# Where the expert products of a routed feed-forward stand: three ups for two gates in the route, and block 4's ups at fixed places in block 3's end

## The chip, the core and the metric

The kernel runs on one core of a Trainium2 chip. Five engines work side by side, each through its own queue in order: TensorE (PE) multiplies and transposes into PSUM, VectorE (DVE) and ScalarE (ACT) read PSUM and SBUF, GpSimd (POOL) works on SBUF, SyncE (SP) issues DMAs. ACT can issue DMAs too; such an issue stands in ACT's queue like any other instruction. Engines wait for one another through semaphores. The metric is the device time of one execution in microseconds. Three runs of the kernel before took 1309.42, 1313.48 and 1315.73 us; the median is 1313.48.

## What is computed

Four blocks one after the other on x, 2 sequences of 1024 tokens with 128 features, each with a residual: two attention layers with a feed-forward, two local attention layers with a gated feed-forward, one attention with local heads and a latent path mixed by a gate (block 3), and a routed feed-forward of 64 experts with 32 hidden units each (block 4). The change touches the end of block 3 and the first half of block 4. Cut to that:

```python
# block 3, end
gate = jax.nn.sigmoid(local @ gl_w + remote_h @ gr_w)
mixed = gate * local + (1.0 - gate) * remote_h
x = x + (mixed @ out_w + out_b)

# block 4, on the layernorm of x
router_scores = jax.nn.softmax(xt @ Wr + br, axis=-1)        # 2048 tokens x 64 experts
order = jnp.argsort(-router_scores, axis=0)                  # tokens sorted for each expert
group_score = sorted_vals.reshape(Tq, 64, En).sum(axis=1)    # groups of 64 sorted tokens
_, top_flat = jax.lax.top_k(group_score.reshape(-1), Tq * 16)
fs = jnp.where(mask, router_scores, 0.0)                     # scores of the chosen groups
fs = fs / (fs.sum(axis=-1, keepdims=True) + 1e-06)
up = jnp.einsum('td,edh->teh', xt, Wup) + bup
gate = jnp.einsum('td,edh->teh', xt, Wgate) + bgate
h = jax.nn.silu(up) * gate * fs[:, :, None]
out = jnp.einsum('teh,ehd->td', h, Wdown) + fs @ bdown
```

`up` and `gate` do not depend on the routing, so they can be computed while the routing sorts and searches. `h` needs the routing's result, and `out` needs `h`.

## The kernel before

The matmuls and vector operations are written out by hand in the order in which each engine shall take them; in blocks 3 and 4 no scheduler moves them.

**Block 3** runs in beats. `both` (L1030) makes four beats; in each it lets the `Pipe` (L109) run what is due, then one of the score, transpose and value steps of the attention tiles, then one step of `front.todo`, the sort passes that are ready. `Pipe.later(beats, f, bank, rank)` sets a step some beats ahead; with `bank` true it moves on to the next beat that is free for a PSUM bank; within a beat, steps run by rank, lower first. When all eight heads' values of a tile are there, `finish` (L1260) copies them to SBUF (`oT`, L1263) and sets `rest`, which transposes them back (L1270) and normalises them (L1273, L1276). When a group of tiles is complete, `gate` (L1360) weighs local against remote (L1375 to L1399), transposes (L1406), multiplies by the output weights (L1412) and adds to `xo` (L494). For the very last group (`last`) these steps run on DVE at once. Then `Front.tiles` (L1477) normalises the new tokens for block 4: statistics on DVE (L166, L167), the root on POOL (L168 to L171), the scaling (L173) on POOL, on DVE for the last group only. It goes on to transposes (L1490) copied into `xTd` (L1491), router scores (L1496, L1503 to L1507), exp (L1510), softmax weights (L1515 to L1517), transposes of these (L1530), and their copy with a sign into `r_zab` (L1534), from which the sort begins. Each group adds its sort passes to `front.todo`; a pass is a maximum (L1460) and a minimum (L1461) on DVE.

When the tile loop is over, a drain loop calls `both` with a list `todo`: nothing for nine beats, then `ex.up(2)` in six of nine beats. These are the first 12 of the experts' 64 ups.

**The experts' first half** (`Experts`, L1560): there are 64 ups and 64 gates, each one matmul of 128 columns by 512 tokens in float32 (two PE instructions in the trace, L1597). An up is passed through silu on ACT into `hid` (L1606). A gate stays in its PSUM bank until DVE multiplies it into `hid` (L1620); I call this the product. In the route four banks of PSUM, `big`, serve ups and gates. `feed` keeps up to three gates ahead of DVE (four once the ups are gone). `fill(n)` n times issues one product, one up and what `feed` finds room for.

**The route** (`route`, L1741) is a chain on DVE with `fill` calls set into it: the rest of `front.todo`, first 128- and 256-wide passes, then (L1780) ten 512-wide passes, a swap of the two halves by two DMAs (L1786 on SP, L1787 on ACT's queue) and its use at L1793, four more 512-wide passes (L1795), group sums and minima (L1807, L1816), a search in five steps (L1826, whose costly part is L1831), small selections with short PE operations in between (L1849, L1862 to L1864, L1882, L1892), two comparisons over all scores (L1906, L1907), a running sum (the scan L1914) and the masking of the scores (L1919 to L1927). `split` (L1755) cuts the scores into three bfloat16 parts on the way (L1758 on ACT, L1761 on DVE). Only when the masks are there does the second half of block 4 begin: totals (L1683), weighing (L1656, L1660), down (L1672) and the stores.

Of the kernel before, what the change touches and what calls it, by code (L numbers as in the profile page):

```python
# [31 lines left out]
NB = 2  # L32
MT = S // P
# [934 lines left out]
class BlockC:  # L968
# [27 lines left out]
    def run(self):  # L996
        pipe = self.pipe

        def latent():
            self.latent_keys(0)  # L1000
            self.prep(1, 0, 6, lambda: self.prep(1, 1, 10, lambda: self.latent_keys(1)))

        self.prep(0, 0, 1)
        self.prep(0, 1, 9, latent)
        while pipe.now < 8:
            pipe.beat()
        tiles = [(b, at + i) for at, n in self.GROUPS for b in range(NB) for i in range(n)]
        self.mask(*tiles[0])
        for n, (b, m) in enumerate(tiles):
            if m > 4 and m % 2:  # L1010
                self.latent(b, m - 1)
            for ip in range(2):
                nxt = tiles[n + 1] if ip and n + 1 < len(tiles) else None
                self.both(b, m, ip, nxt)

        turn = itertools.cycle(("s0", "s1"))

        def bank():
            for tag in turn:
                wide = self.k.ps_c.tile([P, 1024], F32, tag=tag, name=self.k.name("big"))  # L1020
                yield wide[:, :512]
                yield wide[:, 512:]

        self.ex.bank = bank().__next__
        up, none = lambda: self.ex.up(2), lambda: None
        todo = [none] * 9 + [up, up, none, up, up, none, none, up, up]
        while self.turns or self.values or pipe.due:
            self.both(todo=todo)

    def both(self, b=None, m=None, ip=None, nxt=None, todo=None):  # L1030

        now = self.score(b, m, ip) if m is not None else []
        todo = todo if todo is not None else []
        for i in range(4):
            self.pipe.beat()
            for f in now[i : i + 1] + self.turns[i : i + 1] + self.values[i : i + 1]:
                f()
            if nxt and i == 0:
                self.mask(*nxt)
            for fs in (self.front.todo, todo):  # L1040
                for f in fs[:1]:
                    f()
                del fs[:1]
        for f in self.values[4:]:
            self.pipe.later(0, f)
        self.values = self.turns[4:]
# [213 lines left out]
    def finish(self, b, m):  # L1260
# [18 lines left out]
            )  # L1279
            self.done(b, m)  # L1280

        self.pipe.later(1, rest, True)

    def latent(self, b, m):

# [71 lines left out]
            (2, True, out),  # L1357
        )

    def gate(self, b, j):  # L1360

        k, nc, st = self.k, self.k.nc, self.st[b]
# [20 lines left out]
        def sums():  # L1383
            for i in range(2):
                nc.vector.tensor_reduce(gs[:, i, : n * 16], pws[i], AX.X, ALU.add)
            nc.vector.tensor_tensor(g, g, gs[:, 1, : n * 16], ALU.add)
            if last:
                tanh()
                eng.tensor_tensor(local, local, remote, ALU.subtract)

        def tanh():
            nc.scalar.activation(g, g, AF.Tanh, scale=0.5)
# [16 lines left out]
        def out():  # L1409
            ps = k.mm()  # L1410
            for i in range(n):
                nc.tensor.matmul(  # L1412
                    ps[:, i * D : (i + 1) * D], mT[:, i * P : (i + 1) * P], k.c_out,
                    start=True, stop=True,
                )
            add_tiles(k, k.xo[:, b * MT + at : b * MT + at + n], ps[:, : n * D])
            self.front.tiles(self.pipe, b, at, n)

        beats = (0, 0, 1, 1, 1) if last else (1, 2, 1, 3, 2)
        steps = ((False, products), (False, sums), (False, mix), (True, features), (True, out))  # L1420
# [43 lines left out]
class Front:  # L1464
# [12 lines left out]
    def tiles(self, pipe, b, at, n):  # L1477
# [2 lines left out]
        t = slice(b * MT + at, b * MT + at + n)  # L1480
        xn = w.tile([P, 4, D], F32, tag="xnd", name=k.name("xn"))[:, :n]
        last = (b, at) == (NB - 1, 6)
        norm_tiles(k, w, k.xo[:, t], xn, n, nc.vector if last else nc.gpsimd)
        cut = self.xT[:, b * S + at * P : b * S + (at + n) * P]
        sc = self.sc[:, at : at + n, b, :]

# [73 lines left out]
class Experts:  # L1560
# [6 lines left out]
    def __init__(self, k, xT, own):  # L1567
# [2 lines left out]
        self.parts = [(tp, h) for tp in range(2) for h in range(NB)]  # L1570
        self.units = [(tp, h, c) for tp, h in self.parts for c in range(8)]
        halves = [(unit, e) for unit in self.units for e in range(2)]
        self.ups, self.gates, self.ready = list(halves), list(halves), []

    def new(self):
        n, k = len(self.hid), self.k
# [48 lines left out]
    def fill(self, n=1):  # L1625

        for _ in range(n):
            if self.ready:
                self.ready.pop(0)()
                self.up()  # L1630
                self.feed()


# [107 lines left out]
def route(k, p1, front, fill):  # L1741
# [5 lines left out]
    nc = k.nc  # L1747
# [19 lines left out]
    for n, f in enumerate(front.todo):  # L1767
# [3 lines left out]
            next(first)  # L1771
        elif left == 6:
            next(second)
        fill(n % 2 if left < 10 else n % 3 > 0)

    za, zb = zab[:, 1, :], zab[:, 0, :]

# [2 lines left out]
    j = 512  # L1780
    while j >= 1:
        sort_pass(k, za, zb, 1024, j, j == 512)
        fill()
        za, zb = zb, za
        j //= 2
    nc.sync.dma_start(zb[:64, :], za[64:, :])  # L1786
# [8 lines left out]
    j = 512  # L1795
    while j >= 64:
        sort_pass(k, za, zb, 1024, j, False)
        fill()
        za, zb = zb, za
        j //= 2  # L1800

# [24 lines left out]
    for step in (8, 4, 2, 1, 0):  # L1826
# [2 lines left out]
            pick, k.sm("lrank", 0, 16), n, gs, ALU.is_equal, ALU.mult, accum_out=piv  # L1829
        )  # L1830
        nc.vector.tensor_scalar(junk, every, piv, None, ALU.is_gt, ALU.add, accum_out=above)  # L1831
        fill()
        if step:
            nxt = step // 2 if step > 1 else 1

# [11 lines left out]
    nc.vector.tensor_tensor(piv, piv, above, ALU.add)  # L1847
    ps = k.tr()
    nc.tensor.transpose(ps[:, :P], piv.to_broadcast([P, P]), k.ident)  # L1849
    fill(3)  # L1850
    nc.vector.tensor_reduce(low, ps[:, :P], AX.X, ALU.min)


# [8 lines left out]
    nc.tensor.matmul(ps[:, :2], k.mat["ones"], cnt, start=True, stop=True)  # L1862
    nc.tensor.matmul(ps[:, 2:18], k.mat["tri"], eq, start=True, stop=True)
    nc.tensor.matmul(ps[:, 18:34], k.mat["blk"], eq, start=True, stop=True)  # L1864
    fill(3)
    cs = new([P, 34], "cs")
    nc.vector.tensor_copy(cs, ps[:, :34])
    inc = new([P, 16], "inc")
# [11 lines left out]

    ps = k.mm()
    nc.tensor.matmul(ps[:, :1], k.mat["pair"], cnt[:, 0:1], start=True, stop=True)  # L1882
    fill(3)
    num = new([P, 1], "num")
    nc.vector.tensor_copy(num, ps[:, :1])
    thr = new([P, 1], "thr")
# [6 lines left out]
    none = new([P, 1], "none")  # L1893
    nc.vector.tensor_scalar(none, num, 0.0, 9.0, ALU.is_equal, ALU.mult)
    v = new([P, 1], "v")
    fill(3)
    both = junk[:, :P]
    nc.vector.scalar_tensor_tensor(
        both, ps[:, :P], 1.0, k.mat["pair"], ALU.mult, ALU.mult, accum_out=v
# [270 lines left out]
```

## Time and profile before

One execution was profiled. Its own time is 1315.62 us; the span from the first to the last instruction is 1313.7 us.

| what | us |
|---|---|
| time of the profiled execution | 1315.62 |
| busy over the span: PE, DVE, ACT, POOL | 1153.0, 867.7, 645.3, 485.6 |
| last output transposes of block 3 (L1270) start | 1070.09 |
| sign copy L1534 starts | 1093.02 |
| first product L1620 starts | 1099.64 |
| first 512-wide pass starts | 1138.60 |
| scan L1914 starts | 1219.52 |
| totals L1683 start on PE | 1226.07 |

Busy time of the end, by stage, of the same execution (us):

| stretch | length | PE | DVE | ACT | granted PE clock |
|---|---|---|---|---|---|
| 1000 to 1066, last attention tiles | 66 | 56.8 | 57.5 | 41.9 | 0.95 |
| 1066 to 1092, end of block 3 | 26 | 18.9 | 17.3 | 14.6 | 0.87 |
| 1092 to 1142, 128- and 256-wide passes | 50 | 39.4 | 48.5 | 16.8 | 0.93 |
| 1142 to 1176, 512-wide passes | 34 | 33.7 | 33.2 | 14.7 | 1.00 |
| 1176 to 1194, search | 18 | 13.8 | 17.4 | 5.6 | 1.00 |
| 1194 to 1226, selection, scan, masks | 32 | 24.0 | 25.9 | 5.5 | 0.96 |
| 1226 to 1314, second half of block 4 | 88 | 83.4 | 48.2 | 0.0 | 0.96 |

How to read such views: busy time of PE is modelled at its end, since matmuls overlap, so the distance from one start to the next says more than the duration. An engine takes its queue in order, so a wait at one instruction holds everything behind it. A wait is put down to the engine that released it last. The granted clock is the share of full speed that PE's clock was given in a stretch.

### The profile page before, as it was taken

How to read it: one execution, taken by the hardware profiler on the slowest of the kernel's cores; microseconds unless marked ns; L12 is line 12 of the kernel's file. 1: busy time of each engine (PE TensorE's matmuls, PEld its weight loads, DVE VectorE, ACT ScalarE, POOL GpSimd, SP SyncE). 2: the span in 40 equal slices, each digit the busy share in tenths (PEclk: the TensorE clock that was granted, in tenths of full speed). 3: DMA queues.
4: the chain of work that ended last, by engine and by line, in shares of the span. 5: the costliest groups of instructions: out<-in, count | busy, mean ns of one | idle time of the engine just before them, and what ended most of it. 6: DMA issues, size and time to landing. Idle time of an engine off the chain costs nothing.

```text
span 1313.7 us, 23414 instructions
## 1 busy us (share of the span) xinstructions
PE 1153.0 (88%) x9381; PEld 742.0 (56%) x9441; DVE 867.7 (66%) x1787; ACT 645.3 (49%) x1212; POOL 485.6 (37%) x559
## 2 busy tenths in 40 slices
PE   5899999997588999989989877989999967898798
PEld 3566666665345666656666634545555532243698
DVE  5566666645267776775776625656677969998763
ACT  5454545543245765655655635656665753342000
POOL 1523333223478886675786542222222210000000
PEclk9999999999799999999999988989998988999899
DMA  9000000000011100010101012000000000000000
GB/s 292 1 1 1 1 1 2 1 1 1 9 25 25 26 22 17 22 26 13 24 21 24 6 41 76 2 1 1 1 1 2 1 1 1 0 17 0 25 17 17
DMA packets 19840, 25.18 MB, mean 19 GB/s; under 512 B 2762, under 2 KB 13716, under 8 KB 19476
## 3 DMA queue, kind: packets, MB, share of 16 engines
q1 hardware_dynamic: 19076, 23.02, 6.3%
q8 instruction: 75, 1.23, 0.4%
q10 hardware_dynamic: 656, 0.66, 0.2%
q14 instruction: 33, 0.27, 0.1%
HBM read 13.32 MB, written 1.05 MB: 11 GB/s over the span
## 4 chain that ended last, share of the span: by engine, by line
PE 59%; DVE 23%; ACT 7%; POOL 5%; issue 5%; DMA 0%; DVEq 0%; POOLq 0%; ACTq 0%
PE big L1597 6%; PE mm L1672 4%; PE bank L403 4%; PE s L368 4%; PE bank L904 4%; PE qk L679 3%; PE bank L453 2%; PE s L1206 2%; PE s L779 2%; PE bank L824 2%; DVE nm L1211 2%; PE bank L471 2%; PE tr L1243 2%; DVE nm L374 2%; PE bank L391 2%
## 5 line engine op out<-in xcount | busy, mean ns | idle before, releaser
L724 POOL TENSOR_TENSOR t<-raw,tab 128x512 f32<-128x512 f32 x64 | 80.5, 1282 | 88.3 <-DVE raw L715 84.9
L1211 DVE TENSOR_REDUCE nm<-s 128x4 f32<-128x1024 f32 (+1 forms) x64 | 71.0, 1151 | 60.3 <-PE s L1206 60.0
L374 DVE TENSOR_REDUCE nm<-s 128x1 f32<-128x1024 f32 x64 | 75.1, 1216 | 51.9 <-PE s L368 51.9
L1244 ACT COPY pT<-tr 128x512 f32<-128x512 f32 x120 | 70.0, 597 | 73.2 <-PE tr L1243 73.0
L687 ACT ACTIVATE sq<-qk 128x1024 f32<-128x1024 f32 x32 | 32.7, 1023 | 97.0 <-PE qk L679 97.0
L1243 PE MATMUL tr<-ident,pr 128*128 128x128 f32 x480 | 77.1, 284 | 2.6 <-ACT pT L1244 2.3
L1606 ACT ACTIVATE hid<-big,cols 128x512 f32<-128x512 f32 x62 | 41.9, 686 | 75.8 <-PE big L1597 75.8
L737 POOL TENSOR_TENSOR raw<-raw,t 128x1024 f32<-128x1024 f32 x32 | 75.7, 2365 | 1.9
L731 POOL TENSOR_TENSOR raw<-raw,tab 128x1024 f32<-128x1024 f32 x32 | 75.4, 2355 | 2.5
L1597 PE MATMUL big<-xTd,d_gate 128*128 128x512 f32 x128 | 66.1, 610 | 11.1 <-ACT hid L1606 7.5
L1597 PE MATMUL big<-xTd,d_up 128*128 128x512 f32 x128 | 70.6, 643 | 5.3 <-DVE hid L1620 3.2
L380 ACT ACTIVATE pr<-s,nm 128x1024 f32<-128x1024 f32 x64 | 71.1, 1120 | 7.4 <-DVE nm L374 7.3
L679 PE MATMUL qk<-b_wqkv,hT 128*128 128x512 f32 x128 | 66.4, 643 | 9.4 <-POOL hT L640 5.4
L391 PEld LDWEIGHTS bank<-ident,pr 128*128 128x128 f32 x512 | 56.1, 141 | 30.1 <-issue 22.5
L403 PE MATMUL bank<-pT,v 128*64 128x128 f32 x1024 | 71.7, 284 | 0.7 <-DVE pT L396 0.2
L394 ACT COPY pT<-bank 128x512 f32<-128x512 f32 x64 | 34.9, 587 | 69.1 <-PE bank L391 69.1
L403 PEld LDWEIGHTS bank<-pT,v 128*64 128x64 f32 x1024 | 56.2, 139 | 22.1 <-issue 10.7
L1243 PEld LDWEIGHTS tr<-ident,pr 128*128 128x128 f32 x480 | 54.6, 144 | 21.2 <-issue 11.8
L368 PE MATMUL s<-kk,q 64*128 64x512 f32 x256 | 65.5, 622 | 0.6 <-ACT pr L380 0.5
L391 PE MATMUL bank<-ident,pr 128*128 128x128 f32 x512 | 65.3, 276 | 0.0
L1672 PEld LDWEIGHTS mm<-d_down,hid 128*128 128x128 f32 x496 | 60.4, 194 | 5.7 <-DVE xo L1703 1.9
L1672 PE MATMUL mm<-d_down,hid 128*128 128x128 f32 x496 | 61.1, 278 | 1.3 <-DVE xo L1703 1.3
(359 smaller groups left out, 2809.7 us busy)
## 6 DMA issues: line engine op xcount, KB each, us to landing
vs<-v SPq DMA_DIRECT2D x60, 130.0 KB, 2.2
b_wqkv<-in_L_ffn_wqkv_dram SPq DMA_DIRECT2D x2, 768.0 KB, 8.9
b_tab<-in_c_xpos_dram SPq DMA_DIRECT2D x1, 1024.0 KB, 7.9
d_up<-in_L_ffn_Wup_dram SPq DMA_DIRECT2D x1, 1024.0 KB, 5.2
d_gate<-in_L_ffn_Wgate_dram SPq DMA_DIRECT2D x1, 1024.0 KB, 9.1
out_dram<-xo SPq DMA_DIRECT2D x3, 256.0 KB, 2.3
rows<-in_rows_dram SPq DMA_DIRECT2D x1, 760.0 KB, 7.1
b_w<-in_L_ffn_w_dram SPq DMA_DIRECT2D x2, 341.0 KB, 7.2
```

Source lines behind the costliest of these rows:

```text
L368: nc.tensor.matmul(t["s"][h][:, keys], q[rows, qt * P : (qt + 1) * P], kk[rows, keys], start=True, stop=True,)
L374: nc.vector.tensor_reduce(t["nm"][h], t["s"][h], AX.X, ALU.max, negate=True)
L391: nc.tensor.transpose(ps[:, i * P : (i + 1) * P], t["pr", h][:, at : at + P], k.ident)
L403: nc.tensor.matmul(t["u"][h * 64 : h * 64 + 64, :P], v[:, kb, h * 64 : h * 64 + 64], t["pT"][:, h, kb], start=(kb == 0), stop=(kb == MT - 1),)
L679: nc.tensor.matmul(qk[:, cut], lhsT, k.b_wqkv[:, l, cut], start=True, stop=True)
L724: nc.gpsimd.tensor_tensor(t2[:, :, :, a : a + 32], r4[:, :, :, z : z + 32], self.tabs[l][1][:, m, :, None, a : a + 32].to_broadcast([P, 2, ...
L731: nc.gpsimd.tensor_tensor(r4, r4, self.tabs[l][0][:, m, :, None, :].to_broadcast([P, 2, 8, 64]), ALU.mult)
L737: nc.gpsimd.tensor_tensor(flat, flat, t["t2"].rearrange("p j h d -> p (j h d)"), ALU.add)
L1211: nc.vector.tensor_reduce(nm[h], view[h], AX.X, ALU.max, negate=True)
L1243: nc.tensor.transpose(ps[:, c * P : (c + 1) * P], pr[:, c, t * P : (t + 1) * P], k.ident)
L1597: self.k.nc.tensor.matmul(ps, weights[:, rows], self.xT[:, cut], start=True, stop=True)
L1672: nc.tensor.matmul(sums[part][:, cols], hid[tp, h, c][:, e, cols], k.d_down[:, c + 8 * e, :], start=start and e == 0, stop=False,)
```

## The change

1. The drain loop's list is gone. The 12 ups of block 3's end are set at fixed places instead: four behind the gate sums of the last group, four behind its output, and two each four and five beats later with rank 1, which is behind the transposes and scores due in these beats.
2. `rest` gets rank -1, ahead of all else in its beat, and for the last tile it no longer looks for a free beat.
3. The scaling L173 is on DVE for the last group of both sequences (`at == 6`), not of the second alone.
4. `fill` issues two ups with every odd product and one with every even one, so three ups for two gates.
5. The counts of `fill` along the route: two steps in three also in the last nine steps of `front.todo` (one in two before), one and two in turn in the 512-wide passes (one before), two in each search step (one before), two where the selections had three.

No matmul and no vector operation is added or removed; the scaling of one group moves from POOL to DVE.

```diff
--- before.py
+++ after.py
@@ -1022,25 +1022,21 @@
                 yield wide[:, 512:]
 
         self.ex.bank = bank().__next__
-        up, none = lambda: self.ex.up(2), lambda: None
-        todo = [none] * 9 + [up, up, none, up, up, none, none, up, up]
         while self.turns or self.values or pipe.due:
-            self.both(todo=todo)
-
-    def both(self, b=None, m=None, ip=None, nxt=None, todo=None):
+            self.both()
+
+    def both(self, b=None, m=None, ip=None, nxt=None):
 
         now = self.score(b, m, ip) if m is not None else []
-        todo = todo if todo is not None else []
         for i in range(4):
             self.pipe.beat()
             for f in now[i : i + 1] + self.turns[i : i + 1] + self.values[i : i + 1]:
                 f()
             if nxt and i == 0:
                 self.mask(*nxt)
-            for fs in (self.front.todo, todo):
-                for f in fs[:1]:
-                    f()
-                del fs[:1]
+            for f in self.front.todo[:1]:
+                f()
+            del self.front.todo[:1]
         for f in self.values[4:]:
             self.pipe.later(0, f)
         self.values = self.turns[4:]
@@ -1279,7 +1275,7 @@
             )
             self.done(b, m)
 
-        self.pipe.later(1, rest, True)
+        self.pipe.later(1, rest, (b, m) != (NB - 1, MT - 1), -1)
 
     def latent(self, b, m):
 
@@ -1356,6 +1352,10 @@
             (1, True, score), (1, False, exp), (1, True, turn), (2, True, value), (2, True, across),
             (2, True, out),
         )
+
+    def ups(self):
+        for _ in range(2):
+            self.ex.up(2)
 
     def gate(self, b, j):
 
@@ -1387,6 +1387,7 @@
             if last:
                 tanh()
                 eng.tensor_tensor(local, local, remote, ALU.subtract)
+                self.ups()
 
         def tanh():
             nc.scalar.activation(g, g, AF.Tanh, scale=0.5)
@@ -1415,6 +1416,11 @@
                 )
             add_tiles(k, k.xo[:, b * MT + at : b * MT + at + n], ps[:, : n * D])
             self.front.tiles(self.pipe, b, at, n)
+            if last:
+
+                self.ups()
+                for beats in (4, 5):
+                    self.pipe.later(beats, lambda: self.ex.up(2), False, 1)
 
         beats = (0, 0, 1, 1, 1) if last else (1, 2, 1, 3, 2)
         steps = ((False, products), (False, sums), (False, mix), (True, features), (True, out))
@@ -1480,7 +1486,7 @@
         t = slice(b * MT + at, b * MT + at + n)
         xn = w.tile([P, 4, D], F32, tag="xnd", name=k.name("xn"))[:, :n]
         last = (b, at) == (NB - 1, 6)
-        norm_tiles(k, w, k.xo[:, t], xn, n, nc.vector if last else nc.gpsimd)
+        norm_tiles(k, w, k.xo[:, t], xn, n, nc.vector if at == 6 else nc.gpsimd)
         cut = self.xT[:, b * S + at * P : b * S + (at + n) * P]
         sc = self.sc[:, at : at + n, b, :]
 
@@ -1570,7 +1576,7 @@
         self.parts = [(tp, h) for tp in range(2) for h in range(NB)]
         self.units = [(tp, h, c) for tp, h in self.parts for c in range(8)]
         halves = [(unit, e) for unit in self.units for e in range(2)]
-        self.ups, self.gates, self.ready = list(halves), list(halves), []
+        self.ups, self.gates, self.ready, self.filled = list(halves), list(halves), [], 0
 
     def new(self):
         n, k = len(self.hid), self.k
@@ -1627,7 +1633,8 @@
         for _ in range(n):
             if self.ready:
                 self.ready.pop(0)()
-                self.up()
+                self.filled += 1
+                self.up(1 + self.filled % 2)
                 self.feed()
 
 
@@ -1771,7 +1778,7 @@
             next(first)
         elif left == 6:
             next(second)
-        fill(n % 2 if left < 10 else n % 3 > 0)
+        fill(n % 3 > 0)
 
     za, zb = zab[:, 1, :], zab[:, 0, :]
 
@@ -1780,7 +1787,7 @@
     j = 512
     while j >= 1:
         sort_pass(k, za, zb, 1024, j, j == 512)
-        fill()
+        fill(1 + j.bit_length() % 2)
         za, zb = zb, za
         j //= 2
     nc.sync.dma_start(zb[:64, :], za[64:, :])
@@ -1795,7 +1802,7 @@
     j = 512
     while j >= 64:
         sort_pass(k, za, zb, 1024, j, False)
-        fill()
+        fill(1 + j.bit_length() % 2)
         za, zb = zb, za
         j //= 2
 
@@ -1829,7 +1836,7 @@
             pick, k.sm("lrank", 0, 16), n, gs, ALU.is_equal, ALU.mult, accum_out=piv
         )
         nc.vector.tensor_scalar(junk, every, piv, None, ALU.is_gt, ALU.add, accum_out=above)
-        fill()
+        fill(2)
         if step:
             nxt = step // 2 if step > 1 else 1
 
@@ -1847,7 +1854,7 @@
     nc.vector.tensor_tensor(piv, piv, above, ALU.add)
     ps = k.tr()
     nc.tensor.transpose(ps[:, :P], piv.to_broadcast([P, P]), k.ident)
-    fill(3)
+    fill(2)
     nc.vector.tensor_reduce(low, ps[:, :P], AX.X, ALU.min)
 
 
@@ -1862,7 +1869,7 @@
     nc.tensor.matmul(ps[:, :2], k.mat["ones"], cnt, start=True, stop=True)
     nc.tensor.matmul(ps[:, 2:18], k.mat["tri"], eq, start=True, stop=True)
     nc.tensor.matmul(ps[:, 18:34], k.mat["blk"], eq, start=True, stop=True)
-    fill(3)
+    fill(2)
     cs = new([P, 34], "cs")
     nc.vector.tensor_copy(cs, ps[:, :34])
     inc = new([P, 16], "inc")
@@ -1880,7 +1887,7 @@
 
     ps = k.mm()
     nc.tensor.matmul(ps[:, :1], k.mat["pair"], cnt[:, 0:1], start=True, stop=True)
-    fill(3)
+    fill(2)
     num = new([P, 1], "num")
     nc.vector.tensor_copy(num, ps[:, :1])
     thr = new([P, 1], "thr")
@@ -1893,7 +1900,7 @@
     none = new([P, 1], "none")
     nc.vector.tensor_scalar(none, num, 0.0, 9.0, ALU.is_equal, ALU.mult)
     v = new([P, 1], "v")
-    fill(3)
+    fill(2)
     both = junk[:, :P]
     nc.vector.scalar_tensor_tensor(
         both, ps[:, :P], 1.0, k.mat["pair"], ALU.mult, ALU.mult, accum_out=v
```

## The prediction

> **What bounds the kernel now.** I read the page first, then busy time by stage, the waits of VectorE (DVE), and the timeline of each engine from 1060 us on. The page gives the frame:
>
> ```profile
> span 1313.7 us, 23414 instructions
> ...
> PE 59%; DVE 23%; ACT 7%; POOL 5%; issue 5%; DMA 0%; DVEq 0%; POOLq 0%; ACTq 0%
> ```
>
> The built orders of both kernels are the same on every engine up to the output transposes of the last tile (about 1062.8 us), so only what follows counts, and the ranks given to earlier output transposes change nothing. Busy time by stage (columns: stretch, length, then busy time and count of PE, PEld, DVE, ACT, POOL; granted clock, DMA share, GB/s):
>
> ```profile
> 1066.00:1084.00 18.00, 12.31 (x32) 6.00 (x33) 10.03 (x38) 10.08 (x15) 2.09 (x5) 0.81 0.00 0
> ...
> 1142.00:1158.00 16.00, 16.00 (x35) 5.77 (x34) 16.00 (x27) 5.50 (x8) 0.00 (x0) 1.00 0.02 4
> ...
> 1194.00:1212.00 18.00, 18.00 (x51) 8.43 (x50) 12.05 (x40) 5.50 (x8) 0.08 (x1) 1.00 0.00 0
> ```
>
> Three regimes: from 1066 neither engine is full (a chain of short steps), at 1142 to 1158 PE and DVE are both full, at 1194 to 1212 PE is full and DVE is not. DVE's waits from 1083 to 1228 us put a price on the last regime:
>
> ```profile
> DVE hid L1620 <- PE big L1597: 5.9, 7, 1.0
> DVE xn L173 <- POOL ln_mn L171: 1.5, 1, 1.5
> ```
>
> **Route, the sum.** From the first gate product (L1620, starting 1099.64) to the scan L1914 (1219.52) is 119.9 us. In it DVE waits 5.9 us for PE, 0.3 us at L1831 and 0.2 us at L1898: 6.4 us. So DVE has 113.5 us of work there. The change neither adds nor removes any of it: 64 gate products, the same passes. It only decides when PE's matmuls stand before a product. Their prices:
>
> ```profile
> 1161.68 1.02 PE L1597 MATMUL big<-xTd,d_gate 128*128 128x512 f32 x2
> 1162.54 1.02 PE L1597 MATMUL big<-xTd,d_up 128*128 128x512 f32 x2
> 1163.40 1.02 PE L1597 MATMUL big<-xTd,d_gate 128*128 128x512 f32 x2
> ```
>
> ```profile
> 1143.53 0.74 DVE L1620 SCALAR_TENSOR_TENSOR hid<-big,cols,hid 128x512 f32<-128x512 f32 x1
> 1144.20 0.68 DVE L1460 TENSOR_TENSOR r_zab<-r_zab 128x512 f32<-128x512 f32 x1
> 1144.80 0.68 DVE L1461 TENSOR_TENSOR r_zab<-r_zab 128x512 f32<-128x512 f32 x1
> 1145.40 0.74 DVE L1620 SCALAR_TENSOR_TENSOR hid<-big,cols,hid 128x512 f32<-128x512 f32 x1
> ```
>
> The first three rows are PE's timeline, the next four DVE's. From start to start, an up or a gate costs PE 0.86 us when nothing holds it (1161.68, 1162.54, 1163.40), a product costs DVE 0.66 and a 512-wide pass 1.20.
>
> Before, each product brings one up and one gate, 1.72 us of PE. After, two products bring three ups and two gates, 2.15 us of PE per product, until the 52 ups left for the route are used up: 34 fills take 51, the 35th the last. The fills of the changed kernel, counted in its built order: 20 while the 128- and 256-wide passes run (18 before, because the last nine steps now fill two times in three), 15 in the ten 512-wide passes (10 before). So **all ups now lie ahead of the end of the 512-wide passes**, and gate 38 stands behind the last of them.
>
> DVE alone would reach gate 38 at: 38.96 us from the first gate to the first 512-wide pass (1138.60 in the trace), plus two more products 1.32, ten passes 12.0, fifteen products 9.9, then two products and one subtraction L1761 (0.60): 64.1 us.
> PE reaches it at: 38 gates and 52 ups less the six that it can issue before the first product (three gates, two ups, a gate; more is barred, since the next up takes the bank of the first gate). That is 84 matmuls, 84 x 0.855 = 71.8 us, starting about 1.4 us after the first product (the six begin cold after L1530, and the two ups share a bank, with a silu of 0.69 between): 73.2 us. So DVE must wait at least 9.1 us there. Going through the fills one by one with these prices, PE also loses 2.1 us in the 128-wide part: with four banks, and up to three of them holding gates, nearly every second fill has an up that takes the bank of the product just being made, so PE cannot work ahead while DVE sorts. Gate 38 then comes at 75.3: **11.2 us of waiting**. Ends: 9.1 and, if every matmul took the 0.95 us seen where ups and gates alternate on tight banks (1142 to 1158), 84 x 0.095 = 8.0 more, 19.2. I take 11.2, since a long PE backlog is the state of the rows above.
>
> After gate 38 only gates are left, 0.86 us of PE against 0.66 plus passes, searches and copies on DVE: no further wait for products. What loses its cover there:
> First the half-swap DMA on ACT's queue, which now stands behind all silus:
>
> ```profile
> 1158.33 0.54 ACTq L1787 DMA_DIRECT2D r_zab<-r_zab  x1
> ```
>
> Its partner on SP landed after 2.9 us. The last silu starts 74.5 us after the first product, the DMA is issued beside it, lands near 77.5 to 78, and L1793 is due at 77.3: 0.5 us (0 to 1). L1758's copies and L1815's behind it on ACT are due later. Second, the tail. The products end two fills earlier, so the transpose before L1898 is bare: 0.6 us by the rows L1887 to L1898 (a PE transpose of 0.27, more when cold, and two handovers); L1867 0.2; L1831 keeps its 0.3. Together 1.1 us. L1915 stays covered by the scan (2.28 us). POOL's memset of the ones waits for the last search only, as before.
>
> Route after: 113.5 + 11.2 + 0.5 + 1.1 = 126.3, **6.4 us more** than 119.9. Behind the scan nothing changes: before, PE stands idle 7.3 us ahead of L1683, so it starts cold in both kernels.
>
> **Block 3's end, the sum.** The rows that set it:
>
> ```profile
> 1070.09 0.60 PE L1270 MATMUL mm<-ident,oT 128*128 128x128 f32 x4
> ...
> 1076.63 3.45 PE L1597 MATMUL big<-xTd,d_up 128*128 128x512 f32 x4
> ...
> 1080.35 1.88 PE L1597 MATMUL big<-xTd,d_up 128*128 128x512 f32 x4
> ...
> 1089.72 1.28 ACT L1510 ACT_TABLE_LOAD   x1
> ...
> 1091.02 0.31 ACT L1510 ACTIVATE sc<-sc 128x128 f32<-128x128 f32 x1
> ```
>
> Before, the last transposes L1270 wait behind L1490 (held by POOL's normalisation) and two ups; after, they start when oT is copied, 1063.45, 6.6 us earlier. What is late next is DVE. The normalisation of block 3's other last group is now on DVE (two operations, 0.52 us, for 1.7 us on POOL), in order, and waits for POOL's L171 until 1065.15; with it the sort passes wait 1.6 us. Then three passes of 0.78: L1273 at 1068.0 (before 1070.73), the gate sums L1386 end at 1070.3. ACT then has the tanh, a table load 1.28 and four silus of 0.63 ahead of the copy L1491: 1074.8. PE stands idle from 1068.0 to 1074.85, since the scores L1496 wait for that copy, and L1406, ready on DVE at 1072.4, is queued behind them. So L1503 comes at 1075.5; with 0.85 for L1503 to L1507 and four passes (2.1) L494 is at 1078.5 (before 1080.56). From L494 to the end of L173 takes 3.5 (1080.56 to 1084.05 in the trace), L1515 to L1517 0.74, eight passes 4.24: L1503 of the last group at 1086.9 (before 1088.15). Then 0.85, four passes, 0.74 and two passes (1.05): the sign copy L1534 at 1091.7 against 1093.02, **1.3 us earlier**. From it to the first product are twelve passes in both. Ends: 3 us earlier, 1 us later, by what one more hold in this chain costs.
>
> Two rules bear on this. "ScalarE: Activation LUTs", section What ACT_TABLE_LOAD costs, puts a switch at 2.66 us, a load of 1.28 and a drain as long again. The rows show the load, 1.28, and the exp 0.02 us after it: no drain. Both kernels have five loads here, but the first now lies ahead of L1491; by the rule that path is 1.4 us longer and the gain nil. I take the row. "TensorE: Matmul & The Clock Gate", Part 1, speaks against a change that leaves PE idle 6.9 us: half clock after an idle window of some 3.4 us, full clock after as much work. The trace agrees: four instructions took 3.45 us after an idle stretch of 3.4, and 1.88 when warm. By it the four ups behind L1412 take about 5.2 us instead of 3.5 and end near 1082.3, by the warm row at 1080.6; the transposes L1490 wait for xn (1081.95) in any case, and DVE sorts until 1086.9. Hidden, in both sums.
>
> **Total:** +6.4 - 1.3 = +5.1 us. On its own profiled execution (span 1313.7, 1.9 us around it, 1315.6) that is 1320.7. This execution lies 2.1 us above the median of the three runs, 1313.5, so I predict 1318.6, 0.4% slower; 0.5% is 6.6 us, about what a measurement tells from no change.
>
> **Rivals.**
> - The forecast, PE late in the 512-wide passes, 1318.6, own range 1314 to 1323: 0.62.
> - Clearly slower: each up and gate keeps the 0.95 us of tight banks also in the backlog. It decides if PE's period stays above 0.87. For it: up pairs need two banks at once, ACT must drain both. Against: in the new order two to three matmuls lie between the uses of a bank, and a silu takes 0.69. 5.1 + 8.0 = 13.1, 1326.6: 0.20.
> - Not slower: the transposes' whole lead of 6.6 us reaches L1534 (if ACT and DVE do not hold the chain), and PE waits for no bank: 5.1 - 5.3 - 2.1 = -2.3, 1311.2. Against it, the silus ahead of L1491: 0.12.
> - Faster: PE's lead covers the burst and its 5.9 us of waits vanish; -5.9 + 1.6 - 1.3 = -5.6, 1307.9, with scatter beyond 0.5% in half the cases. Against it stands the count of 84 matmuls: 0.06.
>
> **How the numbers follow.** A third of the forecast's cases pass +6.6 us (0.20); with the second rival slower is 0.40. Faster takes half the last rival and a third of the third, 0.07; the rest, 0.53, is no change. The range drops the faster tail and the slowest tenth: 1311.5 to 1325.5.
>
> **What would show it.** Right: waits of L1620 for L1597 between the start and end of the 512-wide passes summing to some 10 us, none behind L1793, PE starts 0.86 apart there; L1270 at 1063.5 and L1534 near 1091.7. Wrong: DVE full through the 512-wide passes, or L1534 before 1089 or after 1093.

## The result, and the profile after

The changed kernel takes **1320.2 us** (median of 13 runs, 1316.6 to 1325.2), the kernel before 1314.3 us (median of 13 runs, 1309.4 to 1319.3). The ratio is 1.0046, 95% interval 1.0028 to 1.0063: 5.9 us slower, where 5.1 were forecast on top of 1313.5.

The page of the changed kernel, its span and the chain that ended last:

```profile
span 1317.8 us, 23462 instructions
...
PE 59%; DVE 24%; ACT 7%; POOL 5%; issue 4%; DMA 0%; DVEq 0%; POOLq 0%; ACTq 0%
```

Against the page of before, DVE's share of this chain is up by one point and that of "issue" (time in which the engine waited for nothing that the profile shows) down by one. The page can't say where the 6 us are. Nor do the start times alone: up to the last copy of `oT` (L1263 before, L1259 after) both kernels run the same instructions in the same order, yet that copy starts at 1062.82 us in one profile and at 1060.26 in the other. So I cut the profiles at instructions that all kernels have, and count from that copy. Lines of after are those of before shifted by -4 to +7: the product L1620 is L1626, ups and gates L1597 are L1603, the sign copy L1534 is L1540, the transpose L1849 is L1856.

| stretch, us | before | after | change | forecast |
|---|---|---|---|---|
| last `oT` copy to sign copy (end of block 3) | 30.20 | 28.35 | -1.85 | -1.3 |
| sign copy to first product | 6.62 | 6.62 | 0 | 0 |
| first product to first 512-wide pass | 38.96 | 41.01 | +2.05 | |
| to the use of the swapped halves | 23.16 | 38.49 | +15.33 | |
| to the first search step | 14.40 | 15.59 | +1.19 | |
| to the scan | 43.36 | 33.27 | -10.09 | |
| the last four together (route) | 119.88 | 128.36 | +8.5 | +6.4 |
| scan to end | 94.17 | 94.25 | +0.1 | 0 |

The route's rows show work moved forward: products that stood in the searches now stand in the 512-wide passes. Were that all, the rows would cancel. The waits of DVE in after from 1080 to 1235 us say what is left over (columns: tile, line, what it waited for; us in total, times, longest):

```profile
DVE hid L1626 <- PE big L1603: 12.2, 13, 1.8
DVE r_low L1858 <- PE tr L1856: 1.1, 1, 1.1
DVE r_zab L1905 <- PE tr L1899: 0.4, 1, 0.4
DVE r_cs L1874 <- PE mm L1871: 0.3, 1, 0.3
...
DVE r_zab L1800 <- DMA r_zab<-r_zab: 0.2, 1, 0.2
```

These rows sum to 14.2 us of waiting in the route, where before had 6.4. Of the 12.2 us of product waits, 11.4 lie between 1136 and 1175 us, in the 512-wide passes. One of them, seen on DVE and then on PE:

```profile
1145.24 0.75 DVE L1626 SCALAR_TENSOR_TENSOR hid<-big,cols,hid 128x512 f32<-128x512 f32 x1
...
1147.59 0.75 DVE L1626 SCALAR_TENSOR_TENSOR hid<-big,cols,hid 128x512 f32<-128x512 f32 x1 [1.61 <-PE big L1603]
```

```profile
1145.67 1.02 PE L1603 MATMUL big<-xTd,d_up 128*128 128x512 f32 x2
1146.53 1.02 PE L1603 MATMUL big<-xTd,d_gate 128*128 128x512 f32 x2
1147.39 1.02 PE L1603 MATMUL big<-xTd,d_up 128*128 128x512 f32 x2
1148.25 1.02 PE L1603 MATMUL big<-xTd,d_gate 128*128 128x512 f32 x2
1149.11 1.88 PE L1603 MATMUL big<-xTd,d_up 128*128 128x512 f32 x4
```

The gate that PE began at 1146.53 ends at 1147.55, and the product starts 0.04 us later. PE's starts lie 0.86 us apart without a gap: it is DVE that idles. Busy time by stage shows the same (columns: stretch, length, then busy time and count of PE, PEld, DVE, ACT, POOL; granted clock, DMA share, GB/s), after:

```profile
1095.23:1136.24 41.01, 39.97 (x87) 15.04 (x88) 39.21 (x121) 19.64 (x30) 0.00 (x0) 1.00 0.00 0
1136.24:1174.73 38.49, 38.49 (x91) 17.09 (x90) 26.94 (x41) 18.39 (x28) 0.00 (x0) 1.00 0.07 14
```

In the second row PE is busy for all 38.49 us and DVE for 26.94. In the first row of before, between the first product and the first 512-wide pass, PE had 5 us to spare:

```profile
1099.64:1138.60 38.96, 33.89 (x68) 12.08 (x68) 37.92 (x120) 13.28 (x21) 0.00 (x0) 0.95 0.00 0
```

### The profile page after: what moved, and what is told of

Its sections match the earlier page's. It is cut to its first block, busy times and chain, and to the rows that moved or that the text cites. A ratio compares the mean times of both kernels' runs of the same rounds, so it can differ in the third digit from the quotient of the medians.

```text
span 1317.8 us, 23462 instructions
## 1 busy us (share of the span) xinstructions
PE 1158.3 (88%) x9441; PEld 744.1 (56%) x9441; DVE 869.0 (66%) x1789; ACT 645.7 (49%) x1212; POOL 483.7 (37%) x557
## 4 chain that ended last, share of the span: by engine, by line
PE 59%; DVE 24%; ACT 7%; POOL 5%; issue 4%; DMA 0%; DVEq 0%; POOLq 0%; ACTq 0%
PE big L1603 6%; PE mm L1679 4%; PE bank L403 4%; PE s L368 4%; PE bank L904 4%; PE qk L679 3%; PE s L779 2%; PE s L1202 2%; PE bank L453 2%; PE bank L824 2%; PE s L1198 2%; PE tr L1239 2%; DVE nm L1207 2%; PE bank L471 2%; DVE nm L374 2%
## 5 line engine op out<-in xcount | busy, mean ns | idle before, releaser
L1603 PE MATMUL big<-xTd,d_gate 128*128 128x512 f32 x128 | 67.1, 630 | 14.4 <-DVE hid L1626 12.7
L731 POOL TENSOR_TENSOR raw<-raw,tab 128x1024 f32<-128x1024 f32 x32 | 75.3, 2354 | 2.5
L391 PEld LDWEIGHTS bank<-ident,pr 128*128 128x128 f32 x512 | 56.1, 141 | 30.1 <-issue 22.5
L403 PEld LDWEIGHTS bank<-pT,v 128*64 128x64 f32 x1024 | 57.2, 141 | 22.5 <-issue 11.4
L1603 PE MATMUL big<-xTd,d_up 128*128 128x512 f32 x128 | 63.5, 609 | 1.4 <-ACT hid L1612 0.8
```

Of the source, the lines that this page charges most:

```text
L391: nc.tensor.transpose(ps[:, i * P : (i + 1) * P], t["pr", h][:, at : at + P], k.ident)
L403: nc.tensor.matmul(t["u"][h * 64 : h * 64 + 64, :P], v[:, kb, h * 64 : h * 64 + 64], t["pT"][:, h, kb], start=(kb == 0), stop=(kb == MT - 1),)
L731: nc.gpsimd.tensor_tensor(r4, r4, self.tabs[l][0][:, m, :, None, :].to_broadcast([P, 2, 8, 64]), ALU.mult)
L1603: self.k.nc.tensor.matmul(ps, weights[:, rows], self.xT[:, cut], start=True, stop=True)
```

## Experiments

Each kernel was measured beside the kernel before on one chip, and the ratio is to these runs of before. "End" is the stretch from the last `oT` copy to the sign copy, "route" that from the first product to the scan, both from one profile. The end of e2 and e3, which have before's code there, is 30.8 and 30.7, so two profiles of the same end can differ by 0.6 us; the route of the five kernels with before's route (before, e1, e7, e8, e10) is the same within 0.02.

| kernel | ratio to before (95%) | end, us | route, us |
|---|---|---|---|
| before | 1 | 30.20 | 119.88 |
| after | 1.0046 (1.0028 to 1.0063) | 28.35 | 128.36 |
| e1_end_only | 0.9990 (0.9975 to 1.0005) | 28.34 | 119.88 |
| e2_route_only | 1.0070 (1.0050 to 1.0089) | 30.77 | 127.90 |
| e3_ratio_only | 1.0030 (1.0018 to 1.0042) | 30.66 | 121.99 |
| e4_counts_only | 1.0023 (1.0009 to 1.0037) | 30.21 | 121.93 |
| e6_ratio_early | 0.9949 (0.9930 to 0.9969) | 28.35 | 114.45 |
| e7_ups_late | 0.9964 (0.9951 to 0.9977) | 26.53 | 119.90 |
| e8_scale_pool | 0.9968 (0.9955 to 0.9981) | 26.78 | 119.90 |
| e9_combined | 0.9931 (0.9911 to 0.9951) | 25.47 | 115.87 |
| e10_turns_alone | 0.9964 (0.9947 to 0.9982) | 26.32 | 119.88 |
| e11_ups_behind_exp | 0.9948 (0.9931 to 0.9965) | 28.73 | 114.46 |
| e12_turns_and_early | 0.9920 (0.9889 to 0.9951) | 26.14 | 114.81 |

### The two halves of the change, each alone

e1_end_only keeps the change in block 3 and takes back the route:

```diff
-                self.filled += 1
-                self.up(1 + self.filled % 2)
+                self.up()
...
-        fill(n % 3 > 0)
+        fill(n % 2 if left < 10 else n % 3 > 0)
...
-        fill(1 + j.bit_length() % 2)
+        fill()
```

with before's counts in the searches and the tail too. e2_route_only is the opposite: before's list of ups, ranks and scaling, after's `up` and `fill` lines.

> Only block 3's end is changed (ups at fixed places, output transposes at once, scaling on DVE); the route has the counts and the one-to-one ratio of before. Theory (the loss lies in the route): L1534's counterpart comes 28.4 us after the last oT copy instead of 30.2, waits of the products stay near 6 us, the time is 1.9 us below before, ratio 0.9986. Rival (the loss comes from block 3's end: silus ahead of the copy of xTd, PE cold): slower than before by some 6 us, ratio 1.0046.

> Only the route is changed (three ups for two gates and the new counts of fill); block 3's end is that of before. Theory: products wait some 12 us for PE, the transpose behind the last search step is waited for 1 us, from first product to scan 128.4 us instead of 119.9; 8 us slower than before, ratio 1.006. Rival (the loss is in block 3's end): within 2 us of before.

The end alone gives 0.9990 and 28.34 us, the route alone 1.0070 and 127.90 us. The two add up to the change: -0.10% and +0.70% make +0.60%, against 0.46% measured with an interval from 0.28 to 0.63%. So the loss is in the route, and the end hides part of it: 1.9 us by its stretch, while e1's ratio alone is not clear of no change. The rival that puts the loss in block 3 falls.

### The two halves of the route

e3_ratio_only takes before and adds three ups for two gates; e4_counts_only takes before and adds the new counts of fills.

```diff
-                self.up()
+                self.filled += 1
+                self.up(1 + self.filled % 2)
```

> Three ups for two gates, but the counts of fill of before. Theory (what costs is that all ups and 38 gates must be through PE before the tenth 512-wide pass ends; with the old counts product 38 is due only 74 us after the first, and PE reaches it after 73 to 75): products wait 1 to 3 us in all instead of 5.9, the time is 4 us below before, ratio 0.997. Rival (pairs of ups on four PSUM banks hold PE up wherever they stand): waits as in the changed kernel, 10 us or more, 4 us or more slower than before.

> The new counts of fill, but one up with each product. Theory: 15 products in the ten 512-wide passes bring 30 matmuls, 25.8 to 28.6 us of PE against 21.9 of DVE; some 8 us of waits of products, and about 1.5 us of bare transposes at the tail; 3 to 4 us slower than before, ratio 1.0027. Rival (the ratio alone makes the loss): as before or faster, ratio below 1.0.

e3 missed: a gain of 0.3% was expected, and it lost 0.30%. I had checked PE against DVE at one point, the gate that stands behind the last up, and found DVE later there. The waits of e3 from 1080 to 1235 us:

```profile
DVE hid L1620 <- PE big L1597: 6.0, 7, 1.9
...
DVE r_zab L1832 <- ACT r_every L1816: 2.2, 1, 2.2
DVE r_cs L1868 <- PE mm L1865: 0.6, 1, 0.6
```

The product waits are as many as before's, but earlier, in the 512-wide passes: DVE catches PE before the point that I checked. The second row is a cost that I hadn't listed. It names ACT, but ACT only copies what PE's transposes L1815 leave, and these stand behind the backlog of gates on PE:

```profile
1171.64 2.74 PE L1597 MATMUL big<-xTd,d_gate 128*128 128x512 f32 x6
1174.21 1.04 PE L1815 MATMUL tr<-ident,r_gs 128*128 128x128 f32 x8
1175.82 1.14 PE L1815 MATMUL tr<-ident,r_gs 128*128 128x128 f32 x8 [0.57 <-ACT r_every L1816]
```

e4 lost 0.23% where 0.27% was expected, but not in the places expected: product waits are 4.4 us instead of 8, and the rest is the search's data at L1831 (1.9), `r_cs` (1.4) and L1898 (0.6). Each half alone costs about 2 us of route; both together cost 8. Extra ups and extra products call for PE in the same 512-wide passes: PE is full there in after, and 11.4 us of its product waits lie there.

### Extra ups only where PE has time to spare

e6_ratio_early takes e1 and lets the extra ups come at the first 18 fills alone, those of the 128- and 256-wide passes (set against e1):

```diff
-                self.up()
+                self.filled += 1
+                self.up(1 + (self.filled % 2 if self.filled <= 18 else 0))
```

> After's end of block 3, before's counts of fills, and three ups with two gates only at the first 18 fills (the 128- and 256-wide passes), one to one behind them. Theory (the ups' extra work is free where TensorE has idle time between gates, and costs only when it is spread into the 512-wide passes): by the second swap nine more ups are done than in e1_end_only, so the ups run out before the tail; the waits of the products fall from 5.9 us to 1 to 2 us; ratio to the kernel before 0.996 (0.9945 to 0.9975), about 4 us below e1_end_only. Rival (a fill with three matmul halves more holds the next gate up wherever it stands): product waits stay at 6 us or more, ratio 0.999 or above.

The route falls to 114.45 us, 5.4 below before, and the ratio to 0.9949. The first stage of e6 and its product waits:

```profile
1095.32:1134.32 39.00, 37.98 (x81) 13.93 (x82) 37.96 (x120) 18.65 (x29) 0.00 (x0) 1.00 0.00 0
```

```profile
DVE hid L1626 <- PE big L1603: 1.2, 3, 0.6
```

PE is busy for 37.98 us in a stage that is as long as before's (39.00 against 38.96), where before used 33.89. Nine ups are done in time that was idle, and they no longer stand in PE's queue later: of before's 5.9 us of product waits, 5.3 lay in the selections behind the search (products 49 to 55 of 64), and there e6 has none. So three ups for two gates is no loss by itself. After spread it over all fills, and set more fills beside it.

### The end of block 3, edit by edit

Three kernels take its three edits apart. e7_ups_late is e1 with the four ups of `sums` on later beats (the four behind the last tiles stay, unlike what its expectation says); e8_scale_pool is e1 with the scaling back on POOL; e10_turns_alone is before with nothing but the output transposes at once. The lines of e7 and e8 are set against e1, that of e10 against before.

```diff
e7:
-                self.ups()
...
-                for beats in (4, 5):
+                for beats in (4, 4, 5, 5):
e8:
-        norm_tiles(k, w, k.xo[:, t], xn, n, nc.vector if at == 6 else nc.gpsimd)
+        norm_tiles(k, w, k.xo[:, t], xn, n, nc.vector if last else nc.gpsimd)
e10:
-        self.pipe.later(1, rest, True)
+        self.pipe.later(1, rest, (b, m) != (NB - 1, MT - 1), -1)
```

> e1_end_only with the first four ups taken out of the sums step and of the lines behind the last tiles, and put on beats 4, 4, 5, 5. Theory (the silus and their table loads stand on ScalarE ahead of the copies at L1491 and L1407, and the copies release the last product of the router): the last product's wait goes, from the last oT copy to the last sign 24 to 25 us instead of 28.3, ratio 0.9957 (0.994 to 0.9975). Rival (the chain of VectorE and GpSimd up to the copies sets the end, so that the silus only fill a gap): 28 us and 0.999 as in e1_end_only.

> e1_end_only with the scaling of the first pair of tiles at at = 6's sister group back on GpSimd (only the last group on VectorE). Theory (VectorE stalls 1.5 us at L173 for GpSimd's ln_mn, and what stands behind it on VectorE is late by so much): last oT copy to last sign 26.3 to 26.8 us instead of 28.3, ratio 0.9975 (0.996 to 0.999). Rival (the copy at L1491 behind GpSimd's 1.7 us scaling sets the end): 28.3 us or more, ratio 0.999 to 1.0005.

> The kernel before with one edit of the change alone: the last output transposes (rest) on any beat and ahead of the beat's other steps; the ups stay in before's list, the scaling of the last pair but one stays on GpSimd, the route is before's. Theory (the edit is what shortens the end in after, and the two other edits there give part of it back): VectorE's wait of 4.07 us at L1273 goes, and some of it comes back at the sum L494 behind the ups and at GpSimd's part of the norm; from the last oT copy to the last sign 27 to 28 us instead of 30.2, ratio 0.998 (0.9965 to 0.9995). Rival (the lead is lost in the later waits, and moving the ups is what gained): 30 us, ratio 1.000 (0.9985 to 1.0015).

The waits of DVE between the last `oT` copy and the sign copy, in before, in after and in e10:

```profile
DVE sums L1273 <- PE mm L1270: 4.1, 1, 4.1
DVE xo L494 <- PE mm L1412: 1.7, 1, 1.7
DVE xn L173 <- POOL ln_mn L171: 1.5, 1, 1.5
DVE red L1515 <- ACT sc L1510: 0.3, 1, 0.3
```

```profile
DVE xn L173 <- POOL ln_mn L171: 3.0, 2, 1.5
DVE sc L1509 <- PE mm L1502: 2.6, 1, 2.6
```

```profile
DVE xn L173 <- POOL ln_mn L171: 1.5, 1, 1.5
DVE red L1515 <- ACT sc L1510: 1.2, 1, 1.2
DVE sc L1503 <- PE mm L1496: 1.2, 1, 1.2
```

They sum to 7.6, 5.6 and 3.9 us. Taken from the stretches (30.20, 28.35, 26.32) they leave 22.6, 22.75 and 22.4: the end is some 22.5 us of DVE work plus its waits, and the same holds for e7 (3.8 of waits), e8 (4.4) and e9 (3.2). An edit can bring here just the wait that it takes away, less the waits that it makes. The transposes at once took away the 4.1 us at L1273, and gained 3.9 (whether the free beat or the rank does it was not tried). The two edits beside them gave 2.0 of that back. The scaling on DVE made a second wait at L173, and e8 without it is 1.6 shorter. The early ups made the wait at L1509, which is read on ACT in after:

```profile
1067.62 0.23 ACT L1393 ACTIVATE gs<-gs 128x32 f32<-128x32 f32 x1 [6.78 <-DVE gs L1386]
1067.87 1.28 ACT L1612 ACT_TABLE_LOAD   x1
1069.16 2.42 ACT L1612 ACTIVATE hid<-big,cols 128x512 f32<-128x512 f32 x4
1071.46 0.39 ACT L1497 COPY xTd<-mm 128x256 f32<-128x256 f32 x1
```

The copy to `xTd` had its input since 1065 (L1496 ends at 1065.21) and stands behind the load and four silus until 1071.46; ACT had been idle for 6.78 us ahead of the tanh. e7 takes these silus away: the wait at L1509 goes, and 0.8 us comes in its place at the exp. The stretch is 26.5 us, not the 24 to 25 expected: I had expected more gain than the wait that was there to be removed (2.6). e10 went the other way, 26.3 where 27 to 28 was expected. e8 came out as expected (26.8).

### Better versions

e9_combined puts e6, e7 and e8 together. e11_ups_behind_exp moves its last ups behind the exp:

```diff
-                for beats in (4, 4, 5, 5):
+                for beats in (5, 5, 6, 6):
```

> The three edits of e6_ratio_early, e7_ups_late and e8_scale_pool together. Theory: the gains of the route and of the end add, since they lie behind each other on the same path: oT to sign about 23 us, product waits 1 to 2 us, ratio 0.9925 (0.990 to 0.995). Rival (the four ups that start later are then missing in the route's early passes, so that one gain eats the other): ratio 0.996 or above.

> e9_combined with its last ups on beats 5, 5, 6, 6 instead of 4, 4, 5, 5, so that the last exp stands ahead of the silus on ScalarE. Theory (the exp was late behind two silus and a table load): VectorE's wait of 1.7 us at the sum behind the exp goes, from the last oT copy to the last sign 23.8 us instead of 25.5, ratio 0.992 (0.990 to 0.994). Rival (what the end gains, the first gates lose, since four ups come later): the first products of the route wait 1 us or more longer, ratio as in e9_combined or above, 0.993 to 0.995.

e9 has a ratio in the range expected, 0.9931, though its end is 25.5 us and not 23 (1.7 of it waiting for the exp). Its rival is there in small: the route is 1.4 us longer than e6's, with product waits of 2.6 us where 1 to 2 was expected. The first three gates in e6 and then in e9:

```profile
1089.35 2.84 PE L1603 MATMUL big<-xTd,d_gate 128*128 128x512 f32 x6 [0.95 <-ACT hid L1612]
```

```profile
1088.79 4.30 PE L1602 MATMUL big<-xTd,d_gate 128*128 128x512 f32 x6 [2.38 <-ACT hid L1611]
```

The granted clock in these rows is 1.00 in e6 and 0.64 in e9, and PE ends its last up 1.4 us later in e9's route than in e6's. That the later ups left PE idle for long enough to lower the clock fits the 2.38 us before the row, but was not tried by itself.

e11 missed: its end is 28.7 us and not 23.8. Its ratio, 0.9948, lies in the rival's range, but not for the rival's reason. The exp wait went, and the last wait of the chain took its place, on DVE and on PE:

```profile
1089.54 0.48 DVE L1539 TENSOR_SCALAR r_zab<-mm,small_c 128x256 f32<-128x256 f32 x1 [4.98 <-PE mm L1535]
```

```profile
1083.88 5.40 PE L1602 MATMUL big<-xTd,d_up 128*128 128x512 f32 x8 [2.24 <-ACT hid L1611]
1089.12 0.38 PE L1535 MATMUL mm<-ident,sc 128*128 128x128 f32 x2
```

The last transposes of the router stand behind four ups, and those waited for silus to empty their banks. The first gates, which the rival named, lost nothing (route 114.46).

e12_turns_and_early leaves all that out: before, with e10's line and e6's two lines.

> The kernel before with two edits: the last output transposes at once (e10_turns_alone) and three ups with two gates at the first 18 fills alone (e6_ratio_early); the ups stay in before's list, the scaling on GpSimd, the counts of fills as before. Theory (end and route lie behind each other, and neither needs the other edits): from the last oT copy to the last sign 26.3 us, from the first product to the scan 114.5 us, from the copy to the end 241.5 to 242.5 us against 250.9 before, ratio 0.993 (0.991 to 0.995). Rival (the ups at before's places come too late to feed the early passes): product waits of 4 us or more in the route, 117 us or more from first product to scan, ratio 0.996 or above.

It has the lowest ratio of the study: 1304.9 us against 1314.9, 0.9920 (0.9889 to 0.9951), end 26.14, route 114.81, all close to what was expected. Its product waits in the route:

```profile
DVE hid L1620 <- PE big L1597: 1.6, 3, 0.6
```

The ups at before's places feed the early passes nearly as well as after's (route 114.45 in e6). That e12 also beats e6, e9 or e11 is not shown: their intervals overlap.

## Why the prediction was right, and where it was off

**The main step held.** PE late in the 512-wide passes was forecast at 11.2 us of waits, between 9.1 and 19.2; measured were 12.2, with PE's starts 0.86 us apart. The rival of 0.95 us per matmul in the backlog falls with these rows, and so does the one in which the waits vanish. The last ups stand where the count of fills had put them, with gate 38 behind them:

```profile
1170.57 1.02 PE L1603 MATMUL big<-xTd,d_up 128*128 128x512 f32 x2
1171.42 5.31 PE L1603 MATMUL big<-xTd,d_gate 128*128 128x512 f32 x12
```

```profile
1172.55 0.75 DVE L1626 SCALAR_TENSOR_TENSOR hid<-big,cols,hid 128x512 f32<-128x512 f32 x1 [0.44 <-PE big L1603]
```

The sum had PE through gate 38 at 75.3 us behind the first product, and DVE there at 64.1 without waits. Product 38 starts at 77.3 (1172.55), with 12.2 us of product waits behind DVE: so PE came 1.9 us later than forecast and DVE 1.0, and the waits are 1.0 more than the term. 0.8 us of them is a wait at 1134.79, before the first 512-wide pass. No product waits behind gate 38, as said.

**The tail was mis-sized.** Forecast were 0.6, 0.2 and 0.3 at L1898, L1867 and L1831, 1.1 in all; measured are 0.4, 0.3 and 0, and 1.1 at a place where I had named no cost, the transpose L1849 (L1856 in after), which L1851 waits for. The step that was off is the price of a gate there: the prediction took 0.86 us for each gate after gate 38. PE in after:

```profile
1201.87 1.98 PE L1603 MATMUL big<-xTd,d_gate 128*128 128x512 f32 x4 [2.26 <-DVE hid L1626]
1206.12 3.07 PE L1603 MATMUL big<-xTd,d_gate 128*128 128x512 f32 x4 [2.26 <-DVE hid L1626]
1210.37 3.62 PE L1603 MATMUL big<-xTd,d_gate 128*128 128x512 f32 x4 [1.17 <-DVE hid L1626]
1213.82 0.27 PE L1856 MATMUL tr<-ident,r_piv 128*128 128x128 f32 x1
```

The same two gates take 1.98 us at 1201.87 and 3.62 at 1210.37, and the transpose stands behind them. In these 8 us the granted clock (before the last two columns) is 0.57, and from 1207 to 1213 it is 0.50:

```profile
1206.00:1214.00 8.00, 6.71 (x10) 2.44 (x11) 6.87 (x18) 0.00 (x0) 1.09 (x2) 0.57 0.00 0
```

In before the search ran at 1.00 with ups among the gates and PE busy for 13.8 of 18 us (1176 to 1194). In after the ups are gone by then, PE works 2 us and idles 2.26 in a search step, and the clock falls. e2_route_only has the same order there, and in its profile the slow spell came two search steps earlier, in the second and third of five instead of the fourth and fifth:

```profile
1206.03 3.78 PE L1597 MATMUL big<-xTd,d_gate 128*128 128x512 f32 x4 [1.49 <-DVE hid L1620]
1210.28 1.98 PE L1597 MATMUL big<-xTd,d_gate 128*128 128x512 f32 x4 [0.47 <-DVE hid L1620]
1214.52 1.99 PE L1597 MATMUL big<-xTd,d_gate 128*128 128x512 f32 x4 [2.26 <-DVE hid L1620]
1216.34 0.27 PE L1850 MATMUL tr<-ident,r_piv 128*128 128x128 f32 x1
```

There the transpose came in time, no wait for it appears, and search to scan took 31.91 us instead of 33.27. So, by these two profiles, 1.4 us of after's tail hang on when the clock falls. The prediction had used the clock rule for the end of block 3 and had not asked it of the tail.

**Smaller terms of the route.** The swap DMA behind the silus: 0.5 forecast (0 to 1), 0.2 measured. The waits of after sum to 14.2, of before to 6.4; that explains 7.8 of the 8.5 us. The other 0.7 is spread over DVE's instructions. It would fit that an instruction that waits can't overlap the end of the one ahead of it (a 0.75 us product costs 0.66 from start to start when it needn't wait), at eight more places. The other profiles agree: the route less its waits is 112.8 to 112.9 us with four waits (e6, e12), 113.2 to 113.5 with nine (e3, before), 114.2 with 16 or 17 (e2, after), some 0.1 us for each wait. No kernel was made to test it alone. Term by term, the route's miss of 2.1 us is product waits +1.0, tail +0.7, this +0.7 and the swap -0.3.

**Block 3's end.** -1.3 forecast, -1.85 measured. The transposes began 0.64 us after the copy of `oT` started (0.63 forecast), the wait of DVE at L173 was 1.5 (1.6), PE's idle time ahead of the scores 6.7 (6.9), and tanh, table load and silus stood ahead of the copy as worked out. The rival in which the whole lead of 6.6 us reaches the sign copy falls even without the other edits: 3.9 in e10. The table load was followed by its silu 0.01 us later (1067.87 + 1.28, then 1069.16), so the row was the right choice, and not the 2.66 us of the Trainium skill ("ScalarE: Activation LUTs", What ACT_TABLE_LOAD costs). The four cold ups were estimated at 5.2 us and took 4.69; hidden, as said.

In sum the two misses, 0.55 us more gained in the end and 2.1 more lost in the route, partly cancel: from the `oT` copy to the end of the program the change costs 6.7 us in the profiles where 5.1 were forecast. That the total was met more closely than the route is luck to that extent.

## What to carry to other kernels

- Before more work is put into gaps, find in which stage the engine has them: busy time by stage showed PE with 5 us to spare ahead of the 512-wide passes and none in them, and one condition (18 fills) turned the same edit from a loss of 0.3% (e3 against before) into a gain of 0.4% (e6 against e1).
- When an engine gets a backlog, list everything else in its queue, not only what the backlog is for: the search's transposes and the router's transposes each waited 2 to 5 us behind ups and gates, the `xTd` copy behind silus.
- An earlier start is worth at most the wait that it removes. 22.5 us of DVE work plus its waits gave the length of block 3's end within 0.3 us in each kernel read so, and showed that two of three edits worked against the third.

## What the runs showed of the hardware

- PE's clock fell without a long idle stretch. In after no gap in the searches was over 2.26 us, yet the granted clock was 0.57 from 1206 to 1214. The Trainium skill ("TensorE: Matmul & The Clock Gate", Part 1) ties half clock to an idle window of some 3.4 us, and also tells of a kernel in which short, frequent idle times between groups of matmuls made the clock swing; these traces agree with the second. Divided into six stretches of 4.24 us from the first search step on, the thirteen profiles part in two: in nine kernels PE is busy for 0.60 or more of every stretch, and the clock stays at 1.00; in after, e2, e3 and e4 there are stretches of 0.43 to 0.47, and the clock falls within the first to third of them or right behind. One stretch of before and one of after that still ran at 1.00:

```profile
1188.88:1193.12 4.24, 2.54 (x6) 0.68 (x4) 4.13 (x10) 1.37 (x2) 0.14 (x1) 1.00 0.00 0
```

```profile
1198.80:1203.04 4.24, 1.98 (x5) 0.67 (x4) 4.14 (x8) 0.00 (x0) 0.00 (x0) 1.00 0.00 0
```

The four kernels also have the longer gaps there (up to 2.26 or 2.46 us, against 1.60 in the nine), so share and gap aren't told apart, and no kernel was made to test either.
- The part that no kernel changed varies more than the change is worth. The last `oT` copy started between 1056.05 us (e3) and 1065.55 (e8). Effects of 2 us could be read only from stretches with a common start, and from the medians of many runs.
